# A decoder layer with routed experts: group tasks cut into steps of two sequences and booked by load, other phases, norms on ScalarE, powers for routing

## The chip, the cores and the metric

The kernel runs on one core of one Trainium2 chip. The metric is the device time in microseconds of one execution, from the first to the last instruction with what lies around it. Engines are named as in the profile: PE (matmul) and PEld (its weight loads), DVE, ACT, POOL, and SP, which here only issues DMAs.

## The reference, cut to what matters

```python
def _L0_xattn_ref(x, encoder_output, ...):          # 32 sequences, 128 tokens, D = 128, H = 16, HD = 8
    x = ln(x + attn(x, x, x, sa_..., causal=True), ln1_g, ln1_b)
    x = ln(x + attn(x, enc, enc, ca_..., causal=False), ln2_g, ln2_b)
    x = ln(x + moe(x, router_w, router_b, e_w1, e_b1, e_w2, e_b2), ln3_g, ln3_b)

def moe(x, rw, rb, w1, b1, w2, b2):                   # E = 8 experts, K = 2, FF = 512
    router_weights = softmax(x @ rw + rb)
    topw, topi = top_k(router_weights, 2)
    topw = softmax(topw)
    h = gelu(x @ w1[e] + b1[e])                       # for the chosen experts
    return sum over the two chosen e of topw * (h @ w2[e] + b2[e])
```

Everything is float32.

## The kernel before, in words

The 32 sequences are eight groups of four (`G = 4`), once for self-attention (`s0` to `s7`) and once for cross-attention (`c0` to `c7`). One sequence of one kind is a unit, so there are 64 units. `order` lists them: first `LEAD` units of self-attention alone, then the two kinds in turn, at the end cross-attention alone. Time in the program is counted in half-slots, two for each unit. `half_slot(h)` writes out the work of one: with t = h // 2, half of the scores of unit t (PSUM tile `sc`) and of the transposed scores of unit t - 2 (PSUM tile `st`, interleaved on PE), then the values of unit t - 3 and the transposed maxima of t - 1, or the splitting of the maxima and the outputs of t - 3. `sc` and `st` exist once each (`ps_sc`, `ps_st`). DVE's `m` (L425) reads `sc` and frees it; ACT's exponential `pr` (L433) reads `st` and frees it. For self-attention POOL then masks `pr` (L437).

All that is done for a whole group stands in `table`, a list of calls for each half-slot, executed after the unit's own work. `turn_input` transposes the four sequences (L343, copied by ACT at L349), `keys`, `queries` (one matmul and four ACT activations, L365) and `values_of` project them, `turn_output` and `project` close the attention, `normalize` computes mean and variance on DVE, raises variance plus epsilon to the power -0.5 on POOL (L313, L314), and scales on DVE (L317). `hand_over` gives a self-attention group to cross-attention, `keep_x2` keeps the output of cross-attention. `route` computes the router's softmax (exponentials on ACT at L551 and L567) and the two chosen experts. `place` gives each token its row in the blocks of its expert, and `scatter` writes the rows to DRAM with indirect DMAs from POOL, two for each sequence (L684). The half-slot of each such call is written by hand, relative to the group's first or last unit:

```python
        at(2 * t0 - 4, queries, s)
        at(2 * t3 + 8, turn_output, s)
        steps(2 * t3 + 9, 2, lambda s=s: project(s))
        at(2 * t3 + 12, hand_over, s, c)
```

All instructions stay in the order in which they are written out (`tc.manual_schedule()`), and each engine executes its own in that order.

The experts work in blocks of 128 rows. There are two phases (`PHASES`): the tokens of the first six groups and those of the last two, with 55 and 23 blocks. `Pipeline.run` goes over the blocks: fetch the weights four blocks ahead (578 KB each, on SP's queue, five buffers), first layer on PE, GELU on ACT (L794), second layer of the block before (L805), bias on DVE (L810), and an indirect DMA from POOL that puts the result rows back in the order of tokens (`eo`, L812). The first block comes when the last token of the first phase is scattered (half-slot `start`); the tasks and half-slots that are left then are written out one per block, by `beside`. Also there, `combine` sums for each group the two weighted results of each token and `finish` normalizes and writes the output. The sums of the first phase's six groups begin at the third block of the second phase, two groups at a time; the sums of the second phase's groups come after the last block. A sum's fetch of results (`gt`) waits on SP for all results of its phase that have been issued so far (`ph.done`).

Of the kernel before, what the change touches and what calls it, by code (L numbers as in the profile page):

```python
# [20 lines left out]
E = 8  # L21
# [3 lines left out]
PHASES = ((0, 6), (6, 2))  # L25
# [16 lines left out]
LEAD = 11  # L42
# [19 lines left out]
def kernel(  # L62
# [54 lines left out]
    def fetch(gr):  # L117
        src, n = (x, "xg") if gr.kind == "s" else (enc, "eg")
        gr.src = io.tile(
            [P, G, P], F32, tag=n, name=f"{n}_{gr.gi}", bufs=3 if n == "xg" else 1  # L120
        )
        nc.sync.dma_start(
            out=gr.src, in_=src[G * gr.gi : G * gr.gi + G].rearrange("b p d -> p b d")
        )
# [78 lines left out]
    vs = [const.tile([P, G, H * VS + VC - VS - VW], F32, name=f"v_{i}") for i in range(3)]  # L203
# [24 lines left out]
    nc.gpsimd.memset(mhalf, -0.5)  # L228
    bo_s = row(sa_bo, P, "bo_s")
# [74 lines left out]
    def normalize(y, name):  # L304
# [3 lines left out]
        rs = small.tile([P, G], F32, tag="rs", name=f"rs_{name}")  # L308
        for t in range(G):
            nc.vector.bn_stats(st[:, t, :], y[:, t, :])  # L310
        for t in range(G):
            nc.vector.bn_aggr(mv[:, t, :], st[:, t, :])
        nc.gpsimd.tensor_scalar(rs, mv[:, :, 1], EPS, None, ALU.add)  # L313
        nc.gpsimd.tensor_tensor(rs, rs, mhalf, ALU.pow)  # L314
        yield
        for t in range(G):
            nc.vector.tensor_scalar(  # L317
                y[:, t, :], y[:, t, :], mv[:, t, 0:1], rs[:, t : t + 1], ALU.subtract, ALU.mult
            )
# [20 lines left out]
    def turned(src, name):  # L340
        pt = mm_tile([P, G, P], f"tp_{name}")
        for b in range(G):
            nc.tensor.transpose(pt[:, b, :], src[:, b, :], ident)  # L343
        return pt

    def turn_input(gr):
        pt = turned(gr.src, gr.name)
        gr.kvT = act.tile([P, G, P], F32, tag="kvT", name=f"kvT_{gr.name}", bufs=3)
        nc.scalar.copy(gr.kvT, pt)  # L349
        if gr.kind == "s":  # L350
            gr.qT = gr.kvT

    def keys(gr):
        pk = mm_tile([P, G, P], f"pk_{gr.name}")
        nc.tensor.matmul(pk, lhsT=gr.w.wk, rhs=gr.kvT, start=True, stop=True)
        gr.k = act.tile([P, G, P], F32, tag="k", name=f"k_{gr.name}", bufs=3)
        nc.scalar.activation(gr.k, pk, AF.Identity, bias=gr.w.bk)

    def queries(gr):

        pq = mm_tile([P, G, P], f"pq_{gr.name}")
        nc.tensor.matmul(pq, lhsT=gr.w.wq, rhs=gr.qT, start=True, stop=True)
        gr.qb = act.tile([P, G, 4, P], F32, tag="qb", name=f"qb_{gr.name}", bufs=3)
        for r in range(4):
            nc.scalar.activation(  # L365
                gr.qb[:, :, r, :], pq, AF.Identity,
                bias=gr.w.bqm[:, r : r + 1], scale=hmask[:, r : r + 1],
            )
# [4 lines left out]
    def values_of(gr):  # L373
        pv = mm_tile([P, G, P], f"pv_{gr.name}")
        for b in range(G):
            nc.tensor.matmul(pv[:, b, :], lhsT=gr.kvT[:, b, :], rhs=gr.w.wv, start=True, stop=True)
# [3 lines left out]
        nc.scalar.copy(  # L380
            gr.v[:, :, : H * VS].rearrange("p b (h c) -> p b h c", c=VS)[:, :, :, :HD],
            pv.rearrange("p b (h d) -> p b h d", d=HD),
        )
# [115 lines left out]
    def turn_output(gr):  # L499
        pt = turned(gr.o, f"o_{gr.name}")  # L500
        gr.oT = act.tile([P, G, P], F32, tag="oT", name=f"oT_{gr.name}")
        nc.scalar.copy(gr.oT, pt)

    def project(gr):

        py = mm_tile([P, G, P], f"py_{gr.name}")
        for b in range(G):
            nc.tensor.matmul(py[:, b, :], lhsT=gr.oT[:, b, :], rhs=gr.w.wo, start=True, stop=True)
        gr.y = act.tile([P, G, P], F32, tag="y", name=f"y_{gr.name}", bufs=3)
        nc.vector.tensor_tensor(gr.y, py, gr.resid, ALU.add)  # L510
        yield from normalize(gr.y, gr.name)

    def affineT(gr, i):

        pt = turned(gr.y, f"y_{gr.name}")
        t = act.tile([P, G, P], F32, tag=f"xT{i}", name=f"xT{i}_{gr.gi}")
        nc.scalar.activation(t, pt, AF.Identity, bias=lnbT[i], scale=lngT[i])
        return t

    def hand_over(gr, to):  # L520

        to.qT = affineT(gr, 0)
        to.resid = act.tile([P, G, P], F32, tag="x1", name=f"x1_{gr.gi}", bufs=4)
        nc.gpsimd.tensor_tensor(to.resid, gr.y, bc(lng[0], 1, G), ALU.mult)
        nc.gpsimd.tensor_tensor(to.resid, to.resid, bc(lnb1c, 1, G), ALU.add)

    def keep_x2(gr):
        gr.x2T = affineT(gr, 1)
        gr.x2 = act.tile([P, G, XW], F32, tag="x2", name=f"x2_{gr.gi}", bufs=3)
        x2 = gr.x2[:, :, :P]  # L530
        nc.gpsimd.tensor_tensor(x2, gr.y, bc(lng[1], 1, G), ALU.mult)
        nc.gpsimd.tensor_tensor(x2, x2, bc(lnb[1], 1, G), ALU.add)
# [5 lines left out]
    def route(gr):  # L538
# [12 lines left out]
        nc.scalar.activation(lg, lg, AF.Exp)  # L551
# [15 lines left out]
        nc.scalar.activation(ex, ex, AF.Exp)  # L567
# [110 lines left out]
    def scatter(gr, ph, b):  # L678

        for k in range(2):  # L680

            nc.gpsimd.memset(apart, 0.0)
            t = G * gr.gi + b
            i = nc.gpsimd.indirect_dma_start(  # L684
                out=xs[ph.p][:, :],
                out_offset=bass.IndirectOffsetOnAxis(ap=slots[:, k, t : t + 1], axis=0),
                in_=gr.x2[:, b, :], in_offset=None,
            )
            for j in ph.sent:
                tc.declare_no_dep(i.ins, j.ins, reason="rows of their own")  # L690
            ph.sent.append(i)
# [131 lines left out]
    class Pipeline:  # L823
# [27 lines left out]
        def run(self, beside):  # L851

            self.turn()
            before = None
            for j, (k, i) in enumerate(self.all):
                self.weights(j + AHEAD)
                k.first_layer(i)
                if before:
# [221 lines left out]
```

## Time and profile before

| | us |
|---|---|
| median of 3 timed runs | 776.99 (774.99 to 779.74) |
| the profiled execution | 743.56 |
| its span, first to last instruction | 741.5 |
| PE busy | 596.9 (80%) |
| DVE busy | 421.4 (57%) |
| ACT busy | 347.8 (47%) |
| POOL busy | 364.7 (49%) |
| DMA | 88.06 MB, mean 119 GB/s |

The page's slices cut the span into 40 equal parts of 18.5 us, each digit a share in tenths. A row of a group of instructions ends with the busy time in all, the mean in ns of one instruction, and the idle time of the engine just before them with what ended it. A row of waits says which instruction waited for which: us in total, times, longest.

### The profile page before, as it was taken

How to read it: one execution, taken by the hardware profiler on the slowest of the kernel's cores; microseconds unless marked ns; L12 is line 12 of the kernel's file. 1: busy time of each engine (PE TensorE's matmuls, PEld its weight loads, DVE VectorE, ACT ScalarE, POOL GpSimd, SP SyncE). 2: the span in 40 equal slices, each digit the busy share in tenths (PEclk: the TensorE clock that was granted, in tenths of full speed). 3: DMA queues.
4: the chain of work that ended last, by engine and by line, in shares of the span. 5: the costliest groups of instructions: out<-in, count | busy, mean ns of one | idle time of the engine just before them, and what ended most of it. 6: DMA issues, size and time to landing. Idle time of an engine off the chain costs nothing.

```text
span 741.5 us, 21324 instructions
## 1 busy us (share of the span) xinstructions
PE 596.9 (80%) x8691; PEld 486.4 (66%) x8691; DVE 421.4 (57%) x1313; ACT 347.8 (47%) x671; POOL 364.7 (49%) x744
## 2 busy tenths in 40 slices
PE   5878898789898988888889878856887999875740
PEld 3556566667676766666667666746887999875630
DVE  2354665556776676687587587765522232274466
ACT  3335555465554556456455553533644555432310
POOL 2273555334447536645755633653776555433441
PEclk9798999999989999999999898976999999987975
DMA  6140603920100100100101100153998999979932
GB/s 135 26 98 3 152 22 78 187 35 4 44 2 27 49 2 24 52 2 17 45 3 31 31 2 10 38 179 113 314 309 283 354 355 344 331 252 307 280 122 89
DMA packets 73714, 88.06 MB, mean 119 GB/s; under 512 B 8080, under 2 KB 60336, under 8 KB 73616
## 3 DMA queue, kind: packets, MB, share of 16 engines
q1 hardware_dynamic: 68496, 77.19, 36.2%
q0 software_dynamic: 4544, 9.38, 3.5%
q8 instruction: 68, 1.11, 0.6%
q14 instruction: 30, 0.25, 0.1%
q10 hardware_dynamic: 576, 0.13, 0.1%
HBM read 67.90 MB, written 23.49 MB: 123 GB/s over the span
## 4 chain that ended last, share of the span: by engine, by line
PE 43%; DVE 17%; POOL 13%; DMA 13%; issue 6%; ACT 6%; SPq 1%; DVEq 0%; POOLq 0%
DMA wd<-wpk 7%; POOL xs L684 6%; PE st_s L410 5%; PE ph L789 5%; DVE m_c L425 5%; PE sc_s L397 4%; PE po L805 4%; PE po_s L472 4%; PE st_c L410 3%; DMA eo<-ot,to 3%; PE po_c L472 3%; ACT qb_s L365 3%; DVE m_s L425 2%; PE sc_s L417 2%; PE st_s L402 2%
## 5 line engine op out<-in xcount | busy, mean ns | idle before, releaser
L794 ACT ACTIVATE h<-ph,wd 128x128 f32<-128x128 f32 x312 | 88.8, 368 | 120.6 <-PE ph L789 84.1
L437 POOL TENSOR_SCALAR_AFFINE_SELECT pr_s<-pr_s 128x1024 f32<-128x1024 f32 x64 | 70.0, 1093 | 114.9 <-ACT pr_s L433 114.8
L789 PE MATMUL ph<-xT,wd 128*128 128x128 f32 x624 | 94.2, 298 | 39.6 <-DMA wd<-wpk 30.9
L812 POOL DMA_INDIRECT eo<-ot,to x78 | 77.1, 988 | 99.0 <-DVE ot L810 36.4
L425 DVE TENSOR_REDUCE m_s<-sc_s 128x8 f32<-128x1024 f32 x64 | 78.1, 1221 | 83.8 <-PE st_s L410 67.5
L789 PEld LDWEIGHTS ph<-xT,wd 128*128 128x128 f32 x624 | 83.2, 207 | 46.2 <-DMA wd<-wpk 33.4
L433 ACT ACTIVATE pr_s<-st_s 128x1024 f32<-128x1024 f32 x64 | 65.6, 1025 | 94.0 <-PE st_s L410 88.1
L425 DVE TENSOR_REDUCE m_c<-sc_c 128x8 f32<-128x1024 f32 x64 | 78.0, 1220 | 54.3 <-PE st_c L410 40.9
L433 ACT ACTIVATE pr_c<-st_c 128x1024 f32<-128x1024 f32 x64 | 65.5, 1024 | 63.2 <-PE st_c L410 59.4
L805 PE MATMUL po<-wd,h 128*128 128x128 f32 x624 | 89.1, 290 | 1.9 <-ACT h L794 1.9
L417 PE MATMUL sc_c<-k_c,qb_c 32*128 32x128 f32 x1024 | 78.4, 293 | 9.5 <-DVE m_s L425 5.0
L805 PEld LDWEIGHTS po<-wd,h 128*128 128x128 f32 x624 | 82.8, 206 | 2.1 <-ACT h L794 2.1
L417 PE MATMUL sc_s<-k_s,qb_s 32*128 32x128 f32 x1024 | 82.4, 303 | 0.2 <-ACT qb_s L365 0.2
L410 PE MATMUL st_c<-qb_c,k_c 32*128 32x128 f32 x1024 | 74.9, 282 | 0.0
L410 PEld LDWEIGHTS st_s<-qb_s,k_s 32*128 32x128 f32 x1024 | 73.1, 200 | 1.1 <-issue 1.1
L810 DVE TENSOR_TENSOR ot<-po,wd 128x128 f32<-128x128 f32 x78 | 22.3, 289 | 90.7 <-PE po L805 81.4
L417 PEld LDWEIGHTS sc_c<-k_c,qb_c 32*128 32x128 f32 x1024 | 65.7, 195 | 12.2 <-DVE m_c L425 6.3
L410 PE MATMUL st_s<-qb_s,k_s 32*128 32x128 f32 x1024 | 72.8, 283 | 0.9 <-issue 0.9
L410 PEld LDWEIGHTS st_c<-qb_c,k_c 32*128 32x128 f32 x1024 | 72.3, 195 | 0.5
L684 POOL DMA_INDIRECT xs<-x,slots x64 | 63.8, 997 | 15.7 <-issue 12.0
L417 PEld LDWEIGHTS sc_s<-k_s,qb_s 32*128 32x128 f32 x1024 | 68.8, 202 | 3.1 <-issue 2.1
L397 PE MATMUL sc_s<-causal,ident 128*128 128x512 bf16 x128 | 41.1, 405 | 24.7 <-DVE m_s L425 13.7
(226 smaller groups left out, 1070.4 us busy)
## 6 DMA issues: line engine op xcount, KB each, us to landing
wd<-wpk SPq DMA_DIRECT2D x78, 578.0 KB, 5.3
xt<-xs SPq DMA_DIRECT2D x18, 260.0 KB, 5.2
wpk<-in_L_xattn_e_w_dram SPq DMA_DIRECT2D x16, 256.0 KB, 6.9
gt<-eo SPq DMA_DIRECT2D x8, 512.0 KB, 6.3
xs<-blank_row SPq DMA_DIRECT2D x1, 3575.0 KB
xg<-in_x_dram SPq DMA_DIRECT2D x9, 256.0 KB, 3.3
eg<-in_ctx_dram SPq DMA_DIRECT2D x8, 256.0 KB, 3.5
x2d<-x SPq DMA_DIRECT2D x8, 256.0 KB, 2.5
```

The lines of the kernel that those rows point to most:

```text
L397: nc.tensor.matmul(sc[:, i], lhsT=ident16, rhs=causal, start=True, stop=False)
L410: nc.tensor.matmul(st[:, i, r, :], lhsT=old.group.k[rowsof(g), old.b, :], rhs=old.group.qb[rowsof(g), old.b, r, :], start=False, stop=r == 3,)
L417: nc.tensor.matmul(sc[:, i, r, :], lhsT=new.group.qb[rowsof(g), new.b, r, :], rhs=new.group.k[rowsof(g), new.b, :], start=not new.masked, ...
L425: nc.vector.tensor_reduce(new.m[:, 8 * half : 8 * half + 8], sc.rearrange("p i r k -> p (i r) k"), AX.X, ALU.max,)
L433: nc.scalar.activation(old.pr[:, hs, :], st.rearrange("p i r k -> p (i r) k"), AF.Exp, scale=SCALE)
L437: nc.gpsimd.affine_select(out=old.pr[:, hs, :], in_=old.pr[:, hs, :], pattern=[[0, 8], [1, P]], compare_op=ALU.is_ge, fill=0.0, base=0, ch ...
L472: nc.tensor.matmul(po[VC * r : VC * r + VC, g, :], lhsT=u.group.v[:, u.b, at_v : at_v + VC], rhs=u.pr[:, h, :], start=e == 0, stop=e == 1,)
L684: i = nc.gpsimd.indirect_dma_start(out=xs[ph.p][:, :], out_offset=bass.IndirectOffsetOnAxis(ap=slots[:, k, t : t + 1], axis=0), in_=gr.x2[ ...
L789: nc.tensor.matmul(hid[:, c, :], lhsT=w[:, c * P : (c + 1) * P], rhs=self.xT[i // XB][:, i % XB, :], start=True, stop=True,)
L794: nc.scalar.activation(self.h[i][:, c, :], hid[:, c, :], AF.Gelu, bias=w[:, B1 + c : B1 + c + 1])
L805: nc.tensor.matmul(po, lhsT=h[:, c, :], rhs=w[:, W2 + c * P : W2 + (c + 1) * P], start=c == 0, stop=c == NFC - 1,)
L812: s = nc.gpsimd.indirect_dma_start(out=eo[p][:, :], out_offset=bass.IndirectOffsetOnAxis(ap=self.to[q][:, i % XB : i % XB + 1], axis=0), i ...
```

## The change

The group tasks become generators that do two of the four sequences at each step (`PAIRS`). `book` puts each step in that half-slot of an allowed stretch where the largest of the booked loads of PE, DVE, ACT and POOL is smallest, `chain` keeps the steps of a group in order; the loads (`busy`) are constants in us written in the program. `normalize` scales on ACT (one activation per sequence with the scale and the bias as columns) after two more small operations on POOL. The two exponentials of `route` become powers of e on POOL. `PHASES` is ((0, 5), (5, 3)), which gives 47 and 31 blocks, `LEAD` is 12, the scatters are booked one per half-slot, and each group's sum begins when its blocks are through. Buffers: `xg`, `k`, `qb` and the value tiles from three to four; `gt` takes a buffer of `qb`.

```diff
-PHASES = ((0, 6), (6, 2))
+PHASES = ((0, 5), (5, 3))
-LEAD = 11
+LEAD = 12
...
+    euler = const.tile([P, G, E], F32, name="euler")
+    nc.gpsimd.memset(euler, math.e)
...
         for t in range(G):
             nc.vector.bn_stats(st[:, t, :], y[:, t, :])
+        yield
         for t in range(G):
             nc.vector.bn_aggr(mv[:, t, :], st[:, t, :])
-        nc.gpsimd.tensor_scalar(rs, mv[:, :, 1], EPS, None, ALU.add)
-        nc.gpsimd.tensor_tensor(rs, rs, mhalf, ALU.pow)
-        yield
-        for t in range(G):
-            nc.vector.tensor_scalar(
-                y[:, t, :], y[:, t, :], mv[:, t, 0:1], rs[:, t : t + 1], ALU.subtract, ALU.mult
-            )
+        nc.gpsimd.tensor_scalar(rs[:, 0], mv[:, :, 1], EPS, None, ALU.add)
+        nc.gpsimd.tensor_tensor(rs[:, 0], rs[:, 0], mhalf, ALU.pow)
+        nc.gpsimd.tensor_tensor(rs[:, 1], mv[:, :, 0], rs[:, 0], ALU.mult)
+        nc.gpsimd.tensor_scalar(rs[:, 1], rs[:, 1], -1.0, None, ALU.mult)
+        for pair in range(2):
+            yield
+            for t in (2 * pair, 2 * pair + 1):
+                nc.scalar.activation(
+                    y[:, t, :], y[:, t, :], AF.Identity,
+                    bias=rs[:, 1, t : t + 1], scale=rs[:, 0, t : t + 1],
+                )
...
     def queries(gr):
-        pq = mm_tile([P, G, P], f"pq_{gr.name}")
-        nc.tensor.matmul(pq, lhsT=gr.w.wq, rhs=gr.qT, start=True, stop=True)
-        gr.qb = act.tile([P, G, 4, P], F32, tag="qb", name=f"qb_{gr.name}", bufs=3)
-        for r in range(4):
-            nc.scalar.activation(
-                gr.qb[:, :, r, :], pq, AF.Identity,
-                bias=gr.w.bqm[:, r : r + 1], scale=hmask[:, r : r + 1],
-            )
+        gr.qb = act.tile([P, G, 4, P], F32, tag="qb", name=f"qb_{gr.name}", bufs=4)
+        for ab in PAIRS:
+            pq = pair(f"pq_{gr.name}", ab)
+            nc.tensor.matmul(pq, lhsT=gr.w.wq, rhs=gr.qT[:, ab], start=True, stop=True)
+            for r in range(4):
+                nc.scalar.activation(
+                    gr.qb[:, ab, r, :], pq, AF.Identity,
+                    bias=gr.w.bqm[:, r : r + 1], scale=hmask[:, r : r + 1],
+                )
+            yield
...
-        nc.scalar.activation(lg, lg, AF.Exp)
+        nc.gpsimd.tensor_tensor(lg, euler, lg, ALU.pow)
         yield
         ls = small.tile([P, G], F32, tag="ls", name=f"ls_{gi}")
         nc.vector.tensor_reduce(ls, lg, AX.X, ALU.add)
...
-        nc.scalar.activation(ex, ex, AF.Exp)
+        nc.gpsimd.tensor_tensor(ex, euler[:, :, 0], ex, ALU.pow)
...
+    def book(lo, hi, cost, *call):
+        def then(h):
+            old = busy.get(h, (0.0,) * 4)
+            return max(a + b for a, b in zip(old, cost) if b)
+
+        h = min(range(lo, max(lo, hi) + 1), key=lambda h: (then(h), h))
+        busy[h] = tuple(a + b for a, b in zip(busy.get(h, (0.0,) * 4), cost))
+        return at(h, *call)
...
-        at(2 * t0 - 6, turn_input, s)
-        at(2 * t0 - 5, keys, s)
-        at(2 * t0 - 4, queries, s)
-        at(2 * t0 - 2, values_of, s)
+        chain(
+            h0 - 13, h0 - 2,
+            (lambda s=s: turn_input(s), *TURN),
+            (lambda s=s: keys(s), *TURN),
+            (lambda s=s: queries(s), pe(0.45, 1.6), pe(0.45, 1.6)),
+        )
+        chain(max(h0 - 1, 0) if gi else -2, h0 + 4, (lambda s=s: values_of(s), *TURN))
...
+        route_costs = (pe(0.3, 0.1, 0.9), dve(1.2), dve(1.1), dve(0.8), dve(0.4))
+        ends = chain(ends[9], ends[9] + 5, (lambda c=c: route(c), *route_costs))
...
+        h = ends[3]
+        for b in range(G):
+            for k in range(2):
+                h = book(h, h, pool(1.4), scatter, c, ph, b, k)
+        if gi == PHASES[0][1] - 1:
+            ready = h
...
+    summed = {
+        sum(NBL[:p]) + NS + 2 * G * (n + 1) - 1 + 3: groups["c", PHASES[p][0] + n]
+        for p in range(NP) for n in range(PHASES[p][1])
+    }
...
+        def step(j):
+            if j in summed:
+                sums.append(combine(summed.pop(j)))
+            for a in sums[:2]:
+                if next(a, a) is a:
+                    sums.remove(a)
```

## The prediction

> **What bounds the kernel now.** I read the page's slices first, then the busy times by stage, then PE's waits in the attention stage, then the rows of the operations that the change touches. In the stage rows the columns are: stretch, length, busy us of PE, PE weight loads, DVE, ACT, POOL, then the granted clock, the DMA share and GB/s.
>
> ```profile
> span 741.5 us, 21324 instructions
> PE   5878898789898988888889878856887999875740
> PEclk9798999999989999999999898976999999987975
> 120.00:460.00 340.00, 298.80 (x5397) 229.28 (x5395) 233.19 (x641) 180.46 (x252) 169.22 (x358) 0.93 0.16 35
> 476.00:506.00 30.00, 16.13 (x225) 13.46 (x225) 21.26 (x103) 8.99 (x13) 15.26 (x32) 0.76 0.37 120
> 506.00:580.00 74.00, 63.70 (x500) 60.39 (x501) 27.95 (x135) 38.10 (x119) 46.93 (x88) 0.94 0.84 279
> 580.00:640.00 60.00, 56.44 (x493) 55.12 (x493) 15.80 (x64) 33.13 (x116) 30.55 (x59) 1.00 1.01 349
> 640.00:716.00 76.00, 52.53 (x357) 50.45 (x356) 42.76 (x177) 23.95 (x84) 31.29 (x55) 0.82 0.80 254
> 716.00:742.00 26.00, 0.00 (x0) 0.00 (x0) 12.16 (x47) 0.00 (x0) 4.55 (x7) 0.58 0.36 106
> ```
>
> Four parts. Attention runs to about 476 us and is PE with gaps. From 476 to 506 there is a hole while the last tokens are scattered. From 506 to 716 the 78 expert blocks run, with the DMA engines full in the undisturbed part (1.01 of their time at 349 GB/s). The last 26 us are the sums of the last two groups, PE idle.
>
> The pace of attention: the timeline of ACT has the first of 128 softmax exponentials at 28.81 us and the last at 486.16, one per half-slot, so 457.35 / 127 = 3.60 us per half-slot. What PE itself needs I add up from its timeline between 306 and 319 us, at full clock: a half-slot of self-attention 1.74, of cross-attention 1.29, values 1.08, small transposes 0.4 per sequence; that is 36.1 us for the 16 half-slots of four sequences of both kinds, and the tasks of two groups (transposes, projections, router) 12.7. Together 48.8 / 16 = 3.05 us. The waits of PE between 120 and 460 us say where the rest is (us in total, times, longest):
>
> ```profile
> PE st_c L402 <- ACT pr_s L433: 13.4, 11, 2.1
> PE sc_s L397 <- DVE m_c L425: 9.3, 14, 1.7
> PE sc_c L417 <- DVE m_s L425: 5.0, 3, 1.9
> PE sc_c L417 <- DVE m_c L425: 4.5, 9, 1.1
> PE st_c L402 <- ACT pr_c L433: 3.3, 3, 2.1
> DVE y_c L317 <- POOL rs_c L314: 7.6, 4, 2.2
> ```
>
> The first five are about 36 us in 340 / 3.60 = 94 half-slots. Two PSUM tiles with one buffer each make them: `st` is free once ACT's exponential has read it, `sc` once DVE's maximum has. Either is late when a lump stands ahead of it: on ACT the four query activations (4 x 0.776 = 3.1 us in one half-slot), on DVE the normalization, which also waits for POOL's power (last line).
>
> ```profile
> L314 POOL TENSOR_TENSOR rs_c<-rs_c,mhalf 128x4 f32<-128x4 f32 x8 | 8.4, 1045 | 0.7
> L454 POOL TENSOR_TENSOR m<-m_c,m 128x16 bf16<-128x16 f32 x32 | 7.2, 225 | 2.6
> L531 POOL TENSOR_TENSOR x<-y_c,lng 128x512 f32<-128x512 f32 x8 | 10.2, 1275 | 1.3 <-DVE y_c L317 1.2
> L365 ACT ACTIVATE qb_c<-pq_c,bqmc,hmask 128x512 f32<-128x512 f32 x32 | 22.3, 776 | 6.4 <-PE pq_c L362 6.4
> L479 ACT COPY uT_c<-po_c 128x256 f32<-128x256 f32 x32 | 11.9, 372 | 2.9 <-PE po_c L472 2.5
> L349 ACT COPY kvT_c<-tp_c 128x512 f32<-128x512 f32 x8 | 4.7, 585 | 1.1 <-PE tp_c L343 0.2
> L551 ACT ACT_TABLE_LOAD x1 | 1.3, 1283 | 0.0
> ```
>
> The reader is to see two things here. A copy of half the columns costs 0.372 and not 0.29, so work cut in two gets dearer. And a power of 4 columns takes 1.045 us where another two-input operation of 16 columns takes 0.225.
>
> **What the Trainium skill says.** "ScalarE: Activation LUTs", What ACT_TABLE_LOAD costs: 0.833 ns a column and a fixed part, about 93 ns more for each operand that is a column; a load of another table about 1283 ns. The trace agrees: (585 - 372) / 256 = 0.83 ns, and 1283 ns. "TensorE: Matmul & The Clock Gate", Part 1: PE drops to half clock after a window of some 3.4 us with too little work and needs about as long to come back. The trace agrees in kind: the 32 value matmuls take 1.08 us in one place (308.1) and 1.94 in another (300.8), behind gaps of 2.0 and 0.6 us, and the mean clock of attention is 0.93. "GPSIMD Engine Reference", 3.1: a two-input operation costs about 2.6 cycles an element, with ordinary addition as the example. The rows above give (1275 - 225) / 496 = 2.1 ns, so it fits. No price of a power is stated.
>
> **The change, part by part.**
>
> *Steps of two sequences, spread over half-slots.* The same matmul columns; PSUM reads are cut in two. ACT per 16 half-slots: 8 query activations of 0.776 become 16 of 0.563 (less 256 columns at 0.83), 2.8 us more; ten other reads cut, each 0.16 more, 1.6 us; eight normalization activations of about 0.46 (the 128x128 row of `h` is 0.368, with a second column operand 0.09 more), 3.7 us. ACT goes from 180.46 / 94 = 1.92 to about 2.4 us per half-slot. PE loads weights for some six more matmul pairs, most of it beside a running matmul: 0.06 us a half-slot, 8 in all. POOL gets two operations of about 0.22 per normalization, 1.0 us per 16 half-slots. DVE loses 8 scalings, 3.4 us.
>
> What it buys: a half-slot with queries holds on ACT 1.03 + 4 x 0.563 = 3.3 us instead of 1.03 + 3.1 and often a 0.37 copy, 4.5; PE's own work is 3.1. So of the 16.7 us of waits for ACT two thirds go, 11. The 19 us of waits for DVE lose the normalization and its wait for POOL and keep the routing lumps: 12 go. Together 23 in 94 half-slots, 31 over 128. The clock: 0.93 over 340 us is 48 us at half speed; fewer gaps give back a fifth of the loss, about 4. Against it 8 of PE and about 1 for fuller engines. Net 26 us less.
>
> *Powers for routing.* Two ACT exponentials per group (0.229 and 0.205) go to POOL as powers of 32 and of 4 columns. The order of instructions puts the large one behind the last scatter (1.1) and a product (1.28), and on DVE the sum `ls` of the next half-slot waits for it, with the maximum of the half-slot after that queued behind. Counted from a maximum's end: POOL splits it (0.84), scatters, multiplies, and begins the power at +3.25; DVE reaches `ls` at 3.3 + 0.42 = +3.75. So DVE stalls for the power's length less 0.5, and PE for about 1 us less, since `sc` is usually free that much before PE asks. The length is not in the trace. Lower end 1.05 us: nothing grows with the columns, no stall. Upper end: all above the 0.19 fixed part of a small operation grows, (1.045 - 0.19) / 4 = 0.21 a column, 7.0 us. I take 2.7, the geometric middle: the row of 4 columns can't tell a long start from a long loop. Then PE loses 2.7 - 0.5 - 1 = 1.2 us at each of the five groups routed in attention, 6 us. The upper end: 5.5 x 5 = 27. In exchange ACT needs no exponential between GELUs: two table loads into the exponential and two back, 5.1 us; the first lies in the hole and ACT has slack in the blocks, so 2 us are gained.
>
> *Phases of five and three groups, LEAD 12.* Blocks stay 47 + 31 = 78. The blocks may start at half-slot 136, where it was 137; the eight scatters that gate them come one per half-slot from 128. Before, from half-slot 128 (exponential at 478.5 us, PE work from 476.5) to the first block was 29.5 us. After, POOL has 8 x 1.09 of scatters, 2.6 of products, 1.7 of a normalization, 1 + 2.7 of powers, 16.7 us, then 2.7 to land, 2.8 for the rows, and 4 for transposes and copies: 26.5. Gain 3. What was done ahead then falls beside the first 27 blocks: 24 scatters on POOL instead of 8, 17 us more, and the powers of two groups. POOL holds about 27 x 1.08 + 24 x 1.09 + 22 = 77 us for them, against 27 x 2.5 = 68 that these blocks took. It reaches a block's output up to a few us late; `ot` has four buffers. 3 us lost.
>
> *Sums as soon as a group's blocks are done.* Seven instead of six groups sum beside blocks. In the undisturbed stretch a block takes 2.0 us (10 per 20 us); the 23 blocks beside the six sums took 73 us, so a sum costs (73 - 46) / 6 = 4.5 us. A single one waits on SP for the output just issued (5.2 us to land), and the next weights queue behind it there, with about four blocks fetched ahead as cover: I take the same 4.5, with 3 (its 1 MB at 349 GB/s) and 7 as ends. One more: 4.5 lost. The tail sums one group instead of two: 0.5 MB less to fetch, 1.5 us, and about 3.5 us of DVE work; 5 gained.
>
> Sum: -26 + 6 - 2 - 3 + 3 + 4.5 - 5 = -22.5. The profiled execution took 743.56 us (span 741.5); the timed runs have a median of 776.99, some 33 above it, which no view explains, and I carry the difference over unscaled: 754.5, taken as 754.
>
> **The rivals.**
>
> *A, the forecast: 754.* For it: the waits have the lumps right ahead of them. Against: it rests on a middle price of the power.
>
> *B, the power is proportional, slower: 795.* At 7 us PE stalls 5 x 5.5 = 27, each time long enough for the clock to drop (5 x 1.7, 8 more), the hole grows by 4 where it shrank by 3, and two routings beside blocks hold DVE and POOL, 8. So -26 + 27 + 8 - 2 + 1 + 3 + 8 + 4.5 - 5 = +18.5. For it: the product rows are proportional above 0.19. Against: only that one size was seen. All told a microsecond of power costs about 8 (5 in attention, 3 after), so it decides from 2.7 + 22.5 / 8 = 5.5 us.
>
> *C, cheap power and a smooth stage: 732.* No stall from it (6 back, 1.5 in the hole) and three quarters more of the waits gone, with more clock: -45. For it: 3.05 us of PE work against 3.60. Against: ACT and POOL get fuller.
>
> *D, the lumps only move: 775.* Each half-slot stays at 3.55, since ACT, DVE and POOL all rise or stay near 2.5 and every queue is in order; attention gives 5 instead of 26. That is the change not doing what it says.
>
> **How the numbers follow.** Chances: A 0.43, C 0.23, D 0.13, B 0.21. The range leaves out half of C below and half of B above: 729 to 790. One per cent, about what a measurement of this kernel can tell from no change, is 8 us. Faster: A, C and a little of D, 0.69; same: most of D and the mild edge of B, 0.15; slower: the rest of B, 0.16.
>
> **What would show it.** The row of the power with 32 columns: under 3 us for A, near 7 for B, and DVE's wait of `ls` on it. The exponentials' pace: 3.60 should become 3.4. Waits of `st` on `pr` down by two thirds. No table load on the routing lines. The first block about 26 us after half-slot 128. A tail near 21 us. Wrong would be: waits of ACT's normalization for POOL that hold the exponentials, or weights waiting behind the sums by more than 7 us each.

## The result and the profile after

The changed kernel takes 799.35 us (median of four runs, 797.04 to 801.49) against 776.84 for the kernel before: a ratio of 1.0286, interval 1.0240 to 1.0331. It is slower by 22.5 us, where 754 had been predicted. The profiled execution took 801.49 us, with a span of 799.0. Of all executions below, one (742.33 us, the version with late sums in the fourth set) is over 1.5% above that version's fastest and is left out.

The runs came from several chips, and the unchanged kernel took 742 us on one of them and 775 to 780 on the others. So kernels are compared by their ratio to the kernel before on the same chip, and traces by stage only where they come from chips of one pace.

For that reason the kernel before was traced once more on a chip of the slower pace (the first experiment, called "before, second trace", span 777.5); the trace that the prediction was read from is of the quicker pace. The page of the changed kernel, its slices:

```profile
span 799.0 us, 21713 instructions
PE   6697899899969869869869769765867676679760
PEclk8699899999989989989979899567978789889895
```

PE's row has dips to 6 at every third slice from the 12th to the 24th, which the first trace of before doesn't show, and the clock falls with several of them. The busy time by stage of the changed kernel (stretch, length, busy us of PE, PE weight loads, DVE, ACT and POOL, then the granted clock, the DMA share and GB/s; the stages are start to end attention, the hole before the first block, the blocks, the tail):

```profile
34.00:511.00 477.00, 404.59 (x7196) 314.36 (x7192) 281.02 (x729) 273.09 (x501) 266.54 (x507) 0.92 0.16 35
511.00:529.00 18.00, 6.22 (x52) 3.58 (x50) 6.88 (x46) 5.03 (x9) 10.77 (x23) 0.50 0.67 223
529.00:780.00 251.00, 184.17 (x1374) 176.67 (x1374) 93.38 (x430) 100.10 (x344) 138.56 (x241) 0.85 0.77 250
780.00:799.00 19.00, 0.00 (x0) 0.00 (x0) 5.93 (x20) 3.29 (x8) 4.31 (x9) 0.50 0.21 62
```

The same view of the second trace of before:

```profile
30.00:508.00 478.00, 394.11 (x7102) 305.86 (x7152) 303.71 (x813) 240.97 (x335) 234.22 (x484) 0.94 0.17 37
508.00:529.00 21.00, 7.41 (x65) 5.88 (x65) 12.12 (x72) 3.59 (x6) 10.54 (x22) 0.64 0.55 177
529.00:753.00 224.00, 177.15 (x1346) 171.40 (x1346) 87.32 (x376) 95.00 (x319) 110.22 (x201) 0.87 0.82 271
753.00:777.00 24.00, 0.00 (x0) 0.00 (x0) 11.21 (x44) 0.00 (x0) 3.48 (x5) 0.50 0.40 115
```

With the exact ends (first and last exponential, first matmul of a block, last issue of a scatter of results) the difference of the two spans, 21.5 us, is: start 34.4 instead of 30.1, +4.3; attention 477.0 instead of 477.9, -0.9; the hole 17.8 instead of 20.8, -3.0; blocks 250.8 instead of 224.4, +26.4; tail 19.0 instead of 24.3, -5.3. Attention gained nothing, and the blocks became dearer. The rows of the routing (busy us and mean ns of one; idle time before them and what ended it) say why attention gained nothing:

```profile
L584 POOL TENSOR_TENSOR lg<-euler,lg 128x32 f32<-128x32 f32 x8 | 43.8, 5470 | 3.9 <-DVE lg L583 3.9
L600 POOL TENSOR_TENSOR ex<-euler,ex 128x4 f32<-128x4 f32 x8 | 8.2, 1031 | 0.6
L587 DVE TENSOR_REDUCE ls<-lg 128x4 f32<-128x32 f32 x8 | 1.5, 186 | 49.7 <-POOL lg L584 41.9 <-POOL apart L843 7.8
```

The power of 32 columns takes 5.47 us, twice the 2.7 that the forecast took, and DVE stood 41.9 us in all before the sum `ls` that needs it. One such place, first POOL and then DVE and PE in the timeline (start, length; in brackets the idle time before and its releaser; lines in between are left out):

```profile
276.63 1.09 POOL L459 TENSOR_SCALAR_AFFINE_SELECT pr_s<-pr_s 128x1024 f32<-128x1024 f32 x1
277.68 0.19 POOL L473 CAST m<-m_s 128x16 bf16<-128x16 f32 x1
278.94 1.09 POOL L716 DMA_INDIRECT xs<-x,slots  x1 [0.17 <-issue]
280.07 1.28 POOL L563 TENSOR_TENSOR x<-y_c,lng 128x512 f32<-128x512 f32 x1
281.29 5.48 POOL L584 TENSOR_TENSOR lg<-euler,lg 128x32 f32<-128x32 f32 x1
...
275.09 1.23 DVE L447 TENSOR_REDUCE m_s<-sc_s 128x8 f32<-128x1024 f32 x1 [1.92 <-PE pu_c L508]
286.81 0.19 DVE L587 TENSOR_REDUCE ls<-lg 128x4 f32<-128x32 f32 x1 [7.32 <-POOL lg L584]
288.30 1.21 DVE L447 TENSOR_REDUCE m_c<-sc_c 128x8 f32<-128x1024 f32 x1
...
289.56 1.01 PE L419 MATMUL sc_s<-causal,ident 128*128 128x512 bf16 x2 [5.64 <-DVE m_c L447]
290.90 0.42 PE L432 MATMUL st_s<-qb_s,k_s 32*128 32x128 f32 x2
```

The chain is whole here. A maximum ends at 276.3; POOL begins the power at 281.29, 5.0 us later and not 3.25. The split, the scatter and the product were counted in the 3.25; what was not is that POOL reaches the split only at 277.68, 1.4 us after the maximum, because small operations of a normalization and a mask stand ahead of it. DVE waits 7.32 us for the power; the maximum behind `ls` is late, so PE gets its `sc` back 5.64 us late; and then PE comes back slow: two matmuls in 0.42 us, which take 0.28 again 5 us later. The granted clock was 0.54 from 289.5 to 295.5 us and 1.00 from there to 300.

### The profile page after: what moved, and what is told of

Read it like the earlier page. It is cut to its first block, busy times and chain, and to the rows that moved or that the text cites. A ratio compares the mean times of both kernels' runs of the same rounds, so it can differ in the third digit from the quotient of the medians.

```text
span 799.0 us, 21713 instructions
## 1 busy us (share of the span) xinstructions
PE 617.7 (77%) x8755; PEld 510.7 (64%) x8755; DVE 394.0 (49%) x1233; ACT 394.9 (49%) x891; POOL 427.6 (54%) x811
## 4 chain that ended last, share of the span: by engine, by line
PE 42%; POOL 16%; DVE 15%; DMA 13%; issue 6%; ACT 6%; SPq 1%; another core or an unknown queue 1%; ACTq 0%; POOLq 0%; DVEq 0%
PE st_s L432 6%; POOL lg L584 5%; PE ph L821 5%; DMA eo<-ot,to 5%; PE po L837 4%; DVE m_c L447 4%; PE sc_s L419 4%; DMA wd<-wpk 4%; DVE m_s L447 3%; PE sc_s L439 3%; PE st_c L432 2%; PE st_s L424 2%; PE po_s L494 2%; PE po_c L494 2%; DMA gt<-eo 2%
## 5 line engine op out<-in xcount | busy, mean ns | idle before, releaser
L821 PE MATMUL ph<-xT,wd 128*128 128x128 f32 x624 | 98.4, 308 | 36.8 <-DMA wd<-wpk 23.2
L821 PEld LDWEIGHTS ph<-xT,wd 128*128 128x128 f32 x624 | 88.6, 219 | 41.9 <-DMA wd<-wpk 23.7
L837 PE MATMUL po<-wd,h 128*128 128x128 f32 x624 | 92.7, 296 | 23.1 <-ACT h L826 18.5
L837 PEld LDWEIGHTS po<-wd,h 128*128 128x128 f32 x624 | 85.1, 209 | 25.3 <-ACT h L826 20.6
L439 PE MATMUL sc_s<-k_s,qb_s 32*128 32x128 f32 x1024 | 84.5, 309 | 1.2 <-issue 1.2
L432 PEld LDWEIGHTS st_s<-qb_s,k_s 32*128 32x128 f32 x1024 | 77.0, 210 | 0.0
L432 PE MATMUL st_s<-qb_s,k_s 32*128 32x128 f32 x1024 | 77.0, 294 | 0.0
L439 PEld LDWEIGHTS sc_s<-k_s,qb_s 32*128 32x128 f32 x1024 | 71.1, 208 | 3.9 <-issue 3.9
L432 PE MATMUL st_c<-qb_c,k_c 32*128 32x128 f32 x1024 | 72.1, 279 | 0.0
```

Source lines behind the costliest of these rows:

```text
L432: nc.tensor.matmul(st[:, i, r, :], lhsT=old.group.k[rowsof(g), old.b, :], rhs=old.group.qb[rowsof(g), old.b, r, :], start=False, stop=r == 3,)
L439: nc.tensor.matmul(sc[:, i, r, :], lhsT=new.group.qb[rowsof(g), new.b, r, :], rhs=new.group.k[rowsof(g), new.b, :], start=not new.masked, ...
L821: nc.tensor.matmul(hid[:, c, :], lhsT=w[:, c * P : (c + 1) * P], rhs=self.xT[i // XB][:, i % XB, :], start=True, stop=True,)
L837: nc.tensor.matmul(po, lhsT=h[:, c, :], rhs=w[:, W2 + c * P : W2 + (c + 1) * P], start=c == 0, stop=c == NFC - 1,)
```

## The experiments

**First set of runs, on one chip: is it the powers, or the early sums?** The kernel before once more, for its trace (nothing is edited).

> The kernel before, unchanged, for a second trace: the first one took 743.56 us where its timed runs took 775 to 780, so the two traces differ by 57 us where the times differ by 22. Theory 'that trace was a quick execution': this one takes about 777, and the 33 us more lie in one stage (the expert blocks, where DMA is at its limit, or attention at a lower clock). Theory 'profiled executions of it are quick': about 744 again.

It took 779.55 us with a span of 777.5 (stages above). Attention is longer than in the first trace by 4.5% (477.9 against 457.4), the blocks by 6.3% (224.4 against 211.1), the start by 1.3 us, the hole by 0.7 and the tail by 0.1. So the 33 us between the first profiled execution and the timed runs, which the prediction carried over as a constant, are the pace of the chip and lie mostly in the two long stages.

The change with both exponentials back on ACT:

```diff
-        nc.gpsimd.tensor_tensor(lg, euler, lg, ALU.pow)
+        nc.scalar.activation(lg, lg, AF.Exp)
...
-        nc.gpsimd.tensor_tensor(ex, euler[:, :, 0], ex, ALU.pow)
+        nc.scalar.activation(ex, ex, AF.Exp)
```

> The changed kernel with both exponentials of the routing back on ACT. Theory P (the powers are the loss): the power of 32 columns takes 5.47 us and DVE waits 41.9 us for it; five of the stalls lie in attention at about 5 us of PE and 1 to 2 of clock each, the rest at the hole and the blocks: 30 to 45 us less than 799, so 755 to 770, faster than before. Theory S (the sums among the blocks are the loss, SP holding the weights back behind them): the powers give back only 10 to 15, 785 to 790.

756.12 us, 0.970 (0.9634 to 0.9765): without the powers the rest of the change makes the kernel faster. Its stages:

```profile
34.00:475.00 441.00, 380.64 (x7141) 302.12 (x7191) 285.82 (x735) 273.96 (x513) 233.90 (x502) 0.97 0.19 40
475.00:490.00 15.00, 4.00 (x49) 2.49 (x47) 6.24 (x41) 4.92 (x10) 5.35 (x15) 0.70 0.59 197
490.00:734.00 244.00, 186.35 (x1374) 179.94 (x1374) 95.42 (x428) 111.15 (x356) 124.51 (x236) 0.86 0.80 257
734.00:753.00 19.00, 0.00 (x0) 0.00 (x0) 5.93 (x20) 3.29 (x8) 4.44 (x10) 0.50 0.23 62
```

By span the powers cost 45.7 us: 36.1 in attention (477.0 against 440.9), 2.8 in the hole, 6.3 in the blocks, 0.5 at the start. In attention PE is busy 404.59 instead of 380.64 us with the same matmuls. 55 of 7196 records are missing in the second row, 3 us; so some 21 of the 36 us are not waiting but slower matmuls, and the granted clock agrees, 0.92 against 0.97.

The change with the sums where they stood before (the first phase's from the third block of the second phase on, two at a time, the rest behind the last block), and this with the exponentials on ACT as well:

```diff
-            if j in summed:
-                sums.append(combine(summed.pop(j)))
+            if j == NBL[0] + 2:
+                sums.extend(combine(summed.pop(k)) for k in sorted(summed)[: PHASES[0][1]])
...
-        for j in sorted(summed):
-            step(j)
+        sums.extend(combine(summed.pop(k)) for k in sorted(summed))
```

> The changed kernel with the sums where they were: the five groups of the first phase from the third block of the second phase, two at a time, the other three after the last block. Theory S: SP's 33 us of waiting for result rows goes from the block stage; 15 to 25 us less, less about 8 for a tail of three groups: 785 to 790. Theory P: no gain, 799 to 810, since the tail has three groups instead of one.

> Both of these: exponentials on ACT and the sums late. If the two causes are apart, the two savings add: P and S together 745 to 755; P alone 765 to 780; what the steps of two sequences, the norms on ACT and the phases do for themselves is what is left against the kernel before.

804.02 us, 1.0286 (1.0215 to 1.0357), and 761.83, 0.9774 (0.9707 to 0.9841): where the sums stand makes no difference that the intervals show, with or without the powers. Late sums shorten the blocks (first matmul of a block to last scatter 226.5 us instead of 244.5 without powers) and lengthen the tail by more (41.3 instead of 19.0). The pair with and without powers differs again by 42 us.

**Second set, on the quicker chip (before: 742.28): how do the powers cost so much?** The kernel before with both powers, the edit above turned round:

> The kernel before with only the two exponentials of the routing turned into powers on POOL. Theory P1 (each power of 32 columns holds DVE, and with it the scores, wherever it stands): seven to eight stalls of about 5 us and the clock after them, 25 to 45 us more than before: 805 to 825. Theory P2 (it is the loads booked on POOL in the changed kernel that leave no room for it): 10 us more at most, 780 to 790.

767.04 us, 1.0365 (1.0303 to 1.0427). Powers alone, in the old order, cost 25 us or 3.7%; in the new one 43 on a slower chip, from 0.970 to 1.029. They also cost it elsewhere. Held against the first trace of before, which has the same pace (743.56 us), 12.8 us of the old order's loss lie in attention, 7.6 in the hole and 2.3 in the blocks. By the starts of the same exponentials in both traces, the first five powers cost 4.6 us together, 0.9 each; the rest of attention's share comes at the sixth, which begins at 474.6 us, 25 before the last exponential. In the new order, the changed kernel against the one with exponentials on ACT, the first five cost 34.0, 6.8 each. DVE's waits from 120 to 480 us in the old order (us in total, times, longest):

```profile
DVE ls L556 <- POOL lg L553: 16.2, 5, 3.5
```

3.2 us each; for the changed kernel the same line from 200 to 520 us is

```profile
DVE ls L587 <- POOL lg L584: 37.8, 6, 7.3
```

6.3 each. In the old order nothing stands between POOL's split and the power; in the new one a product does, and from the second power of attention on a scatter too. A wait of 3.2 us was nearly hidden in the old order, one of 6.3 is paid in full. So the spreading and the powers are not independent: the order that fills the half-slots puts work ahead of the power. How much is due to the longer wait and how much to half-slots with less room to hide one was not taken apart.

The change with the consumer of the power two half-slots later, so that DVE's in-order queue doesn't reach `ls` while POOL computes:

```diff
         nc.gpsimd.tensor_tensor(lg, euler, lg, ALU.pow)
         yield
+        yield
+        yield
...
-        ends = chain(ends[9], ends[9] + 5, (lambda c=c: route(c), *route_costs))
+        route_costs = route_costs[:1] + (dve(0.0001), dve(0.0001)) + route_costs[1:]
+        ends = chain(ends[9], ends[9] + 7, (lambda c=c: route(c), *route_costs))
```

> The changed kernel with the powers kept, but the rest of the routing two half-slots later, so that DVE reaches the sum over the powers when POOL should be through. Theory W (DVE's wait in line is the loss, not POOL's 5.47 us as such): most of the 43 us come back, less about 4 for the later start of the blocks: 760 to 770. Theory L (POOL's load is the loss: masks, splits and scatters come late): 785 or more.

763.15 us, 1.0329 (1.0263 to 1.0395): no better than the changed kernel's 1.0286. DVE's wait for `lg` is gone from attention, and PE's waits from 120 to 460 us have a new head:

```profile
PE pm_c L482 <- POOL apart L716: 13.5, 4, 5.2
PE pm_c L482 <- POOL m L476: 7.0, 2, 5.8
PE st_c L424 <- ACT pr_c L455: 6.1, 9, 1.3
PE sc_s L419 <- DVE m_c L447: 5.6, 5, 1.8
```

`pm` is the transpose of the maxima that POOL has split. The split of the next half-slot stands behind the power on POOL, so PE waits for POOL directly, up to 5.8 us. Attention took 446.9 us where a version without powers, on the same chip, took 418.9 (next): 28 us, against 36.1 in the changed kernel on a slower chip. By the starts of the exponentials the first of attention's powers costs 1.0 us now, but the next four still cost 6.2 to 8.2 each, and what was saved goes in the hole, 23.6 us instead of 14.8. The wait moved: POOL's being away for 5.47 us is the cost, since every half-slot needs POOL once; which engine is caught waiting is secondary.

The change without powers and with sums whose fetch waits by name only on the blocks that its group used (written as a dependence in the program, cut down from all blocks done so far):

```diff
-        for j in phases[p].done:
+        n = gr.gi - PHASES[p][0]
+        for j in phases[p].done[: NS + 2 * G * (n + 1) - 1]:
```

> The changed kernel with the exponentials on ACT (756), and each sum's fetch on SP waits only for the result rows of the blocks that hold its group's tokens, not for those of the newest blocks too. Theory S1 (SP stands 30 us in line behind the newest result rows, and the weights with it): the wait falls below 10 us and 8 to 15 us go: 741 to 748. Theory S2 (the fetch would come no earlier to use, DVE's sums and the traffic are the cost): within 4 us of 756.

723.98 us, 0.9794 (0.9734 to 0.9855), no gain over the 0.970 of the version without this edit. The program still held one wait on the newest scatter, and SP's wait for result rows stayed at 32.9 us, so this doesn't test it; the fourth set does.

The change without powers and with the normalization's scaling on DVE, in the same two steps and booked there:

```diff
-        nc.gpsimd.tensor_tensor(rs[:, 1], mv[:, :, 0], rs[:, 0], ALU.mult)
-        nc.gpsimd.tensor_scalar(rs[:, 1], rs[:, 1], -1.0, None, ALU.mult)
...
-                nc.scalar.activation(
-                    y[:, t, :], y[:, t, :], AF.Identity,
-                    bias=rs[:, 1, t : t + 1], scale=rs[:, 0, t : t + 1],
+                nc.vector.tensor_scalar(
+                    y[:, t, :], y[:, t, :], mv[:, t, 0:1], rs[:, 0, t : t + 1],
+                    ALU.subtract, ALU.mult,
```

> The changed kernel with the exponentials on ACT (756), and the scaling of the norms on DVE again in the same two steps, without the two more operations on POOL, booked with their load on DVE. Theory A1 (the norms on ACT relieve DVE, which frees the scores): 5 to 12 us more, 761 to 768. Theory A2 (the spread in steps of two is what counts, the engine of the norms does not): within 4 us of 756; or a little less, as the sums' norm then no longer stands before the GELUs on ACT.

712.71 us, 0.9621 (0.9562 to 0.9680) beside 0.9794 on the same chip; attention 413.0 against 418.9. Norms on ScalarE are no gain either, they cost 1.7% here.

**Third set (before: 775.91): sums and phases, on top of norms on DVE.** The version with norms on DVE, unchanged:

> The kernel with exponentials on ACT and the norms scaled on DVE once more, unchanged, to stand beside the next three on one chip: ratio to the kernel before 0.962 as measured, on a chip where the kernel before takes about 777 perhaps 0.955 to 0.97.

736.54 us, 0.9477 (0.9417 to 0.9536). Sums three blocks later (`- 1 + 6` for `- 1 + 3`, with the edit on the named blocks), and the same with four instead of two blocks between the fetch of a sum's rows and their use (two more `yield` before the first multiply-add of `combine`):

> The same, with each sum starting three blocks later and waiting only for the blocks that hold its group's tokens, so that these rows have long landed when SP comes to the fetch. Each of the seven sums costs 7 to 8 us in the trace of the changed kernel, where the prediction had 4.5. Theory S1 (SP waiting, 33 us in all, starves the weights): the wait goes, each sum costs 4 to 5, 15 to 25 us less than the first of this call, less some 5 for a longer tail. Theory S3 (the wait of DVE for the fetched rows, 45 us, is the cost, since bias and result rows queue behind it): within 6 us of the first, as the fetch still has only two blocks until it is used.

> The kernel of the run before with four blocks instead of two between a sum's fetch and its use on DVE. Theory S3: DVE's 45 us of waiting for the rows falls below 15 and 15 to 25 us go against the first of this call. Theory S1: nothing beyond what the run before gave, within 5 us of it. If both count, 25 to 35 less.

743.10, 0.9567 (0.9512 to 0.9623), and 739.24, 0.9525 (0.9465 to 0.9586): no gain from either. The queue's own waits and DVE's say why, two lines of the first and two of the second:

```profile
SPq L908 <- DMA eo<-ot,to: 33.5, 7, 7.3
DVE acc L922 <- DMA gt<-eo: 49.0, 8, 7.2
```

```profile
SPq L908 <- DMA eo<-ot,to: 36.0, 7, 7.5
DVE acc L924 <- DMA gt<-eo: 19.1, 6, 5.3
```

SP still waited for scatters of results, as in the changed kernel. The reader of the result rows was still held for the newest scatter, since the rows lie in one buffer, so the first of the two had not removed what it meant to remove. The second does show something: DVE's wait for the rows fell by 30 us, SP's stayed, and the time did not move beyond the noise.

Phases of six and two groups instead of five and three (`PHASES = ((0, 6), (6, 2))`), with norms on DVE:

> The first of this call with phases of six and two groups. The blocks start at half-slot 147 instead of 136, with little attention left to fill the time, and fewer tasks fall beside the blocks. Theory F (the tasks left over are what makes the first 24 blocks slow, 8 to 13 us): the hole grows by about 20 us and the blocks give back 10: 8 to 15 us slower. Theory F2 (they cost nothing): 20 slower.

753.64 us, 0.9693 (0.9630 to 0.9756), 17 us slower than 736.54. The first 24 blocks take 71.7 us instead of 87.3, since one group's tasks fewer lie beside them, but the hole before them is 42.9 us instead of 14.6, and that loses more. The phases of five and three are a gain.

**Fourth set (before: 775.05): the wait for the newest scatter.** The version with norms on DVE again, as the reference point, and it with the sums where they stood before:

> The kernel with exponentials on ACT and norms on DVE, sums spread and waiting for the newest rows, to stand beside the other three on one chip: ratio 0.945 to 0.965.

> Exponentials on ACT, norms on DVE, sums where the kernel before had them. If the spread sums are neutral as in the pair with norms on ACT (756 and 762): 0 to 8 us more than the kernel with spread sums, run in this call.

733.62 us, 0.9461 (0.9393 to 0.9529), and 735.47, 0.9452 (0.9394 to 0.9509): the placing of the sums is neutral here too. Next the sums three blocks later and the newest scatter declared independent, since its rows belong to later groups, and this with four blocks between fetch and use:

```diff
-            tc.add_manual_dep(i.ins, j.ins.name, SYNC, reason="results")
+            if n < need:
+                tc.add_manual_dep(i.ins, j.ins.name, SYNC, reason="results")
+            else:
+                tc.declare_no_dep(i.ins, j.ins, reason="rows of later groups")
```

> Exponentials on ACT, norms on DVE, sums three blocks later, and the dependence of a sum's fetch on the result rows of later groups is taken out of the program. In the two earlier tries one wait on the newest result rows had stayed in the program, and SP stood 33 us as before. Theory S1 (SP held behind the newest rows, the weights with it): SP's wait falls below 8 us, a sum costs 4 to 5 instead of 7 to 8, 15 to 22 us less than the kernel that waits, run in this call. Theory S4 (the DMA traffic of a sum and the order of DVE are the cost): within 5 us of it.

> The kernel of the run before with four blocks instead of two between fetch and use. Theory S1: 3 to 8 us less than the run before, as DVE's wait for the rows goes too. Theory S4: no difference.

730.44 us, 0.9428 (0.9364 to 0.9491), and 715.89 us, 0.9241 (0.9174 to 0.9308). The waits of SP and of DVE in the reference point, in the first and in the second of these, one fence each:

```profile
SPq L908 <- DMA eo<-ot,to: 31.9, 11, 10.2
DVE acc L921 <- DMA gt<-eo: 41.2, 8, 7.4
```

```profile
SPq L908 <- DMA eo<-ot,to: 7.7, 1, 7.7
DVE acc L925 <- DMA gt<-eo: 40.2, 8, 6.8
```

```profile
DVE acc L927 <- DMA gt<-eo: 4.0, 1, 4.0
```

Two waits stood in a row. SP's goes first, 31.9 to 7.7 us, and the time moves by 3 us, within the noise, while DVE still waits 40.2 us for rows fetched too late. With both gone the kernel gains 18 us on the reference point, beyond the intervals. Together with the third set, on a chip of the same pace, all four cases of the later sums are there: both waits in place 0.957, DVE's reduced 0.953, SP's reduced 0.943, both 0.924. Of the 3.3% between the first and the last, DVE's wait alone gives 0.4 and SP's alone 1.4. So a sum held the blocks through SP and then again through DVE, and either wait was enough to keep more than half of the loss. This version takes 7.6% less than the kernel before, the lowest ratio of all that ran. Both waits are from the kernel's own order; the changed kernel has them in full (33.0 and 42.2 us).

## Why the prediction was wrong, by its own steps

The terms of its sum, in us, against the traces. "Without powers" is the change with the exponentials on ACT; what it is held against is the second trace of before. The rows on left-over tasks and on sums use the times at which the results of blocks are scattered.

| Step | Predicted | Measured | From |
|---|---|---|---|
| Spread steps, attention | -26 | -37.0 | without powers: 440.9 against 477.9 |
| Powers, attention | +6 | +36.1 | 477.0 against 440.9 |
| Table loads saved | -2 | not measured apart | inside the rows of the powers |
| Hole before the blocks | -3 | -3.0 | counted from the last exponential, with the powers; -5.8 without |
| Left-over tasks beside blocks | +3 | +8.4 | first 24 blocks with late sums, without powers: 81.5 against 73.1 |
| Powers beside blocks | in the 3 above | +6.3 | whole blocks: 250.8 against 244.5 |
| One more sum beside blocks | +4.5 | +11.7 | rest of the blocks' 244.5 against 224.4 |
| Tail | -5 | -5.3 | 19.0 against 24.3 |
| Start | 0 | +4.3 | 34.4 against 30.1 |
| Sum | -22.5 | +21.5 | spans: +21.5 |

**The step that failed is the price of the power**, "I take 2.7, the geometric middle", and the stall worked out from it, "1.2 us at each of the five groups". The row has 5.470 us for 32 columns and 1.031 for 4, so by these two sizes 4.44 / 28 = 0.158 us a column above a fixed 0.4. It grows with the columns, nearer to the upper end that was named (0.21 a column) than to the middle. The prediction held both ends but set its chance by a middle that no row supported. The decision point of rival B, "from 5.5 us", would at 5.47 have given no change. The prediction's own two ends, 41 us between powers of 2.7 and 7, make 9.5 a microsecond and not "about 8", which puts the point at 5.1 and gives +4 at 5.47; the kernel lost 22.5. Two things made a power dearer still in attention. First, the start on POOL was taken as +3.25 after the maximum; it was +3.1 to +5.0 at the first five powers, so that a power of 5.47 us held DVE 6.3 us on average, not the 4.97 that the step "the power's length less 0.5" gives. Second, the clock: attention holds six powers (the sixth begins 6 us before its end), 36.1 us over six is 6.0 each, of which PE's longer busy time, 21 / 6 = 3.5, is the larger part. "TensorE: Matmul & The Clock Gate" in the Trainium skill, Part 1, says that PE falls to half clock after a window of some 3.4 us with too little work and needs about as long to return. The example agrees in kind: after 5.64 us of waiting PE is slow for about 5 us (0.42 us against 0.28 for a pair, granted clock 0.54). The rival had this term, with 1.7 us for each; it was too small. That rival B's 795 lies near the measured 799 is partly luck: its power of 7 us was too long, its gain from the spreading 11 us too small and its price of a sum too low.

**Right in direction: the spreading.** The waits behind the lumps fell as argued, with more to gain in attention than was counted. Activations of 256 columns took 0.572 us, 0.563 predicted, and ACT's normalization 0.488, 0.46 predicted:

```profile
L382 ACT ACTIVATE qb_c<-pq_c,bqmc,hmask 128x256 f32<-128x256 f32 x64 | 30.9, 572 | 0.7 <-PE pq_c L380 0.7
L324 ACT ACTIVATE y_c<-y_c,rs_c 128x128 f32<-128x128 f32 x32 | 14.0, 488 | 16.8 <-POOL apart L843 11.2 <-POOL rs_c L320 3.3 <-POOL apart L714 2.3
```

PE's waits from 120 to 460 us show it where the powers are absent; first before (second trace), then the change with exponentials on ACT:

```profile
PE st_c L402 <- ACT pr_s L433: 20.1, 14, 3.1
PE sc_s L397 <- DVE m_c L425: 19.8, 18, 3.2
```

```profile
PE st_c L424 <- ACT pr_c L455: 8.9, 11, 2.1
PE sc_s L419 <- DVE m_c L447: 8.7, 9, 1.9
PE st_c L424 <- ACT pr_s L455: 3.6, 7, 0.7
```

The largest waits for ACT and for DVE each fell by more than half. In the changed kernel the waits for ACT are as low (3.3 and 3.3 us), and the wait of `sc_s` on DVE is 25.2: what was won is spent on the powers. But the part of the gain that was put down to taking the scaling off DVE was not one: with the scaling back on DVE attention got another 5.9 us shorter. The gain comes from the rest of the change: the halves, the booking, `LEAD` and the added buffers. No run takes these apart, so it is not shown that cutting in two alone makes it.

**The tail** came out to within a microsecond. **The hole's** -3.0 agrees by luck, as it is counted from the last exponential. The prediction counted from half-slot 128; from that exponential to the first block it is 28.4 us before, 30.7 in the changed kernel and 25.8 with exponentials on ACT, so 2.3 more with the powers, where 3 less had been said with powers of 2.7 and 1 in it. (Its items add up to 26.2, not 26.5.) The last three half-slots grew from 7.6 to 12.9 us, and the table has them in attention. **Left-over tasks** were put at POOL's busy time against the time of the blocks, with "a few us late" and 3 us; the 24 blocks took 8 more. Phases of six and two groups give back 16 there and lose more by starting late.

**Sums** were the second term of a wrong size. Part of it was in the reading: the last 23 blocks in the first trace of before take 79 us and not 73, from the scatter of the 55th result to that of the 78th, which by the same sum makes 5.5 each and not 4.5. In the second trace of before, 24 blocks without a sum or left-over task take 50 us, 2.08 each (from the scatter of the 25th block's result, 73 us after the first, to that of the 49th, 123). The last 29 take 95 us, so the six sums beside them cost (95 - 29 x 2.08) / 6 = 5.8 each. In the change with exponentials on ACT the last 53 take 153.3, the first 24 3.3 more than with late sums, so its seven cost (153.3 - 53 x 2.08 + 3.3) / 7 = 6.6. Both lie inside the bounds of 3 and 7, but seven at 6.6 are some 12 more than six at 5.8, and not 4.5. In the best version, with both waits gone, the last 53 take 130 and the first 24 two more than with late sums and norms on DVE (81 against 79): (130 - 110 + 2) / 7 = 3.1 each, about the 3 that the bytes alone were said to need. "The next weights queue behind it" on SP was the right mechanism and half of it; DVE's wait for the same rows, 42.2 us in the changed kernel, was not in the prediction. SP in the changed kernel at one sum:

```profile
632.90 0.76 SPq L906 DMA_DIRECT2D acc<-x2d  x1
...
638.32 0.36 SPq L910 DMA_DIRECT2D gt<-eo  x1
639.50 5.72 SPq L786 DMA_DIRECT2D wd<-wpk  x4
```

Between the two transfers of the sum SP stands 4.7 us for a scatter to land, and the weights of a later block, which waited for nothing of that, go out behind it.

**Table loads** vanish from the routing rows as predicted; what they save was not measured apart from the powers. **The start**, 4.3 us later, was not in the prediction; 3.8 of it are there without the powers, and which of the moved steps does it was not tried.

## What to carry to other kernels

Before an operation is moved to another engine, its price has to be known at the size it will have: a row for one small shape leaves a factor of seven open, and a single run of that operation is cheaper than a guess in the middle. An engine that every step of a pipeline needs once is not free for a long operation because its busy share is low: moving the consumer later moved the wait from DVE to PE and made the kernel no faster. What the operation costs hangs on the order around it, 0.9 us a power in the old one and 6.8 in the new. And where two in-order queues wait for the same transfer in turn, removing one of the waits shows little; take both away before judging.

## What the runs showed of the hardware that was not expected

- By two sizes a power on POOL costs 0.158 us a column and 0.4 fixed (1.031 us for 4 columns, 5.470 for 32), while the ACT exponential of the same 32 columns took 0.229 us before. "GPSIMD Engine Reference", 3.1, in the Trainium skill has about 2.6 cycles an element for an ordinary two-input operation, 2.2 ns at the 1.2 GHz of its example; this case's products agree, (1275 - 225) / 496 = 2.1 ns a column. A power is some 75 times that a column.
- The slow matmuls behind a stall can cost more than the stall: of the 36 us that the powers add to attention, some 21 are longer matmuls at a mean clock of 0.92 instead of 0.97, and only 15 more idle PE.
- The unchanged kernel took 742.28 us on one chip and 775.05 to 779.66 on others, 4.4 to 5% more.
